# Grouped-query scores of a four-layer attention stack: two key heads on the two halves of TensorE's rows instead of one product with zero-padded keys

## The chip, the core and the metric

The kernel runs on one core of a Trainium2 chip. The metric is the device time of one execution, in microseconds (us), as the median of several runs. Durations of single instructions come from one further execution, the profiled one, taken by the hardware profiler. In its lines PE is TensorE's matmul side, PEld its weight loads, DVE is VectorE, ACT is ScalarE, POOL is GpSimd, and SP is the engine whose queue issues the DMAs; a suffix q (SPq, PEq) means the engine's sequencer.

## What is computed

The reference runs four cross-attention layers one after the other on 8 batches of 256 tokens, 512 wide, with a context of 256 tokens per batch. Layer 0 is attention with a feed-forward block, layer 1 is single-head attention, layer 3 is 16-head attention with a gate. The change is in the third of the four, layer 2, grouped-query attention: 32 query heads of 16 dimensions share 8 key/value heads, four query heads to each key head.

```python
q = hidden_state @ Wq + bq;  k = encoder_hidden_state @ Wk + bk;  v = encoder_hidden_state @ Wv + bv
q = q.reshape(b, l, KVH, GROUPS, HD).transpose(0, 2, 3, 1, 4)      # KVH 8, GROUPS 4, HD 16
k = k.reshape(b, s, KVH, HD).transpose(0, 2, 1, 3)
v = v.reshape(b, s, KVH, HD).transpose(0, 2, 1, 3)
scores = jnp.einsum('bkgld,bksd->bkgls', q, k) * scale
scores = scores + encoder_attention_mask[:, :, None, :, :]
attn = jax.nn.softmax(scores, axis=-1)
out = jnp.einsum('bkgls,bksd->bkgld', attn, v)
x = out.transpose(...).reshape(b, l, H) @ Wo + bo + hidden_state   # then a layer norm
```

## The kernel before

**Number format.** Operands of the large products are split into a high and a low part, both in the reduced format fp32r, and a product is the sum of three passes (high·high, high·low, low·high). For the 16 dimensions of a key head the three passes are stacked along the contraction: rows for (q high, k high), (q low, k high), (q high, k low), which makes 3 × 16 = 48 rows for one key head.

**Units.** Layer 2 is worked in 32 units (class `Gqa`), four for each batch; a unit takes two key heads, u = 0 and 1, and the four query heads h of each. It has these parts:

- `load` (L1252, L1253) brings the query tile `qs` (tag stack, 96 rows x 4 x 256) and the key tile `ks` (96 rows x 2 x 256) from the DRAM buffers `q2d` and `k2d`. Row 32·s + 16·u + d holds pass s, key head u, dimension d. In `ks` the columns are two blocks of 256 keys, one for each u, and the rows of the other head are zero in each block. So one product over 96 rows gives, for 128 queries of each head in the weights, 512 columns: 256 scores for u = 0 and 256 for u = 1.
- `A(h)` (L1262) makes the scores with queries on the partitions, only to find row maxima: two products 96x128 by 96x512, one for each half of the queries, each into a PSUM bank of its own (tag sm, two banks). Then DVE (L1272) adds the mask and takes the maximum, four instructions of 128x256.
- `B` (L1293 to L1296) transposes the negated maxima on TensorE, copies them out on ACT and writes them by a DMA, `stack<-mT`, into rows 96 to 99 of `qs`. Rows 96 to 99 of `ks` hold ones for the own head and zeros for the other, so the next product subtracts the maximum.
- `C(i)` (L1315) makes the scores again with keys on the partitions: for i = 0..3 (half of the keys, pair of query heads) one product 100x128 by 100x512 for each u, into the two banks of tag st. DVE (for u = 0) or ACT and POOL (for u = 1) add the mask, and one ACT instruction takes exp.
- `AV` (L636, called from `D`) multiplies the probabilities by the values: sixteen products of 128x32 by 128x512 in fp32, four at a time side by side in four groups of 32 columns of the array. `Burst` keeps them together.

**Order.** `pipeline` runs step t with A of unit t, B of unit t-1, C of unit t-2 and `AV` of an older one; each step has four slots, and in a slot A(i) and C(i) come one right after the other, followed by "fillers": products of layers 1, 2 (projections), and 3 that other generators supply, by a budget of 9 us a step. For the steps 2 to 25 `keep_order` pins TensorE's order to the order of the program; outside them a scheduler with a timeline of its own decides. All DMAs are issued in order by SP's queue.

**Preparation.** `k2d` is four buffers of 96 x 4 x 2 x 256, filled with zeros at the start of the layer: a POOL memset (L1074) of a tile of the ring `ws`, and four DMAs (L1076). `Context.kv` then writes the 16 nonzero rows of each block, six DMAs a batch (L1129). Before the units start, the two `ks` tiles are set to zero (L1557) and their rows of ones are brought by eight DMAs (L1560); rows 96 to 127 of four query tiles are set to zero (L1562).

Of the kernel before, what the change touches and what calls it, by code (L numbers as in the profile page):

```python
# [8 lines left out]
F = mybir.dt.float32  # L9
# [9 lines left out]
P = 128  # L19
# [29 lines left out]
def S(s):  # L49

    o = []
    for p in s.split(","):
# [7 lines left out]
             h="b9-10", xt="c0-3", bc="c4-5", m="c6-8")  # L60
A0_SB = dict(stack="a12-15", wc="a0-1", w8="a2-5", x8="a10-11", at="a6-7", stg="b3,b4,b6",
             P="b5,b0-2", V="v1,v0", vo="b7", nat="b8,b9", h="b10", hc="c0-3", xt="c4-7", bc="c8")
# [13 lines left out]
def tile_xattn_stack(  # L76
# [31 lines left out]
    nc = tc.nc  # L108
# [11 lines left out]
    def nm(s):  # L120
        uid[0] += 1
        return f"{s}_{uid[0]}"
# [40 lines left out]
    def dram(shape, name):  # L163
        return tc.dram_tile(shape, F, name=nm(name))

    def fp(ap):
        return ap.bitcast(F)
# [68 lines left out]
    def feat_mm(pt, ws, ft, xs, n=D):  # L236
        run(feat_steps(pt, ws, ft, xs, n))
        return 12 * n * MMUS

    def tok_mm(pt, xs, tt, ws, n=D):  # L240
        run(tok_steps(pt, xs, tt, ws, n))
        return 12 * n * MMUS
# [236 lines left out]
    v0d = [dram([P, 2, 768], "v0d") for _ in range(NB)]  # L479
    v3d = [dram([P, 2, 768], "v3d") for _ in range(NB)]  # L480


    q2d = [[dram([2, 96, 4, 256], "q2d") for _ in range(2)] for _ in range(NB)]
    k2d = [dram([96, 4, 2, 256], "k2d") for _ in range(4)]
    avd = [[dram([P, D], "avd") for _ in range(4)] for _ in range(NB)]
    med = [dram([P, 2, 2, D], "med") for _ in range(2)]
    wkvd = dram([P, 2, 2, D], "wkvd")
# [25 lines left out]
    for i in range(2):  # L513
        for o, stg, tag in ((wk, sws[i], "wk"), (xs0, sxs[i], "xs")):
            t = ph1.T([P, 2, 2, D], R, tag)
# [29 lines left out]
    def col(name, i):  # L545
        return cols(name)[:, i : i + 1]
# [77 lines left out]
    def flat(t):  # L624
        return fp(t).rearrange("p h t -> p (h t)")
# [215 lines left out]
    def stacks(ph, tag, n):  # L841
        o = []
        for _ in range(n):
            t = ph.T([P, 2, 4, 256], R, tag)
            o += [t[:, 0], t[:, 1]]
        return o
# [215 lines left out]
    ph5, ph6 = Phase(L_SB, PH_PS), Phase(L3_SB, PH_PS)  # L1062
# [5 lines left out]
    for x_ in range(2):  # L1068
        nc.sync.dma_start(
            out=w2od.rearrange("(c r x) n -> x c r n", r=16, x=2)[x_],  # L1070
            in_=w2o.rearrange("(c x r) n -> x c r n", x=2, r=16)[x_],
        )
    zero = ph5.T([96, 2048], F, "ws")
    nc.gpsimd.memset(zero, 0.0)  # L1074
    for t in k2d:
        nc.sync.dma_start(out=t.rearrange("r f u t -> r (f u t)"), in_=zero)  # L1076


    keep = {}

    def kept(tag):
        if tag not in keep:
            keep[tag] = ph5.T([P, WORDS[ph5.sb[tag][0][0]]], F, tag)
        return keep[tag]


    class Context:
# [30 lines left out]
        def kv(self):  # L1118
            b, xs = self.b, self.xs
            pt = ph5.PS("pp")  # L1120
            c = feat_mm(pt, self.wk, 0, xs, n=256)
            nat = ph5.T([P, 2, 2, 256], R, "nat")
            hi, lo = nat[:, 0, 0, :], nat[:, 0, 1, :]
            nc.scalar.activation(hi, pt[:, 0:256], AF.Identity, bias=col("bk2", 0))
            nc.vector.scalar_tensor_tensor(lo, pt[:, 0:256], col("bk2", 0), fp(hi), ALU.add, ALU.subtract)
            for s, j in enumerate((0, 0, 1)):
                for u in range(2):
                    r = 32 * s + 16 * u
                    nc.sync.dma_start(  # L1129
                        out=k2d[b % 4][r : r + 16, :, u, :].rearrange("d f t -> (d f) t"),  # L1130
                        in_=fp(nat[64 * u : 64 * u + 64, 0, j]),
                    )
            yield c
            pt = ph5.PS("pp")
            for kt in range(2):
                c = tok_mm(pt[:, kt * P : (kt + 1) * P], xs, kt, self.wv, n=P)
            tag = ("V", "vb", "va", "V4")[b % 4]
            vo = kept(tag)[:, 1024:] if tag[0] == "v" else kept(tag)
            self.vo = vo.rearrange("p (k v d) -> p k v d", k=2, v=8)
            nc.gpsimd.memset(self.vo[:, :, :, 16:32], 1.0)  # L1140
            for kt in range(2):
                nc.vector.tensor_tensor(
                    self.vo[:, kt, :, 0:16],
                    pt[:, kt * P : (kt + 1) * P].rearrange("p (v d) -> p v d", d=16),
                    bvr.rearrange("p (v d) -> p v d", d=16),
                    ALU.add,
                )
            yield 2 * c
# [90 lines left out]
    class Gqa:  # L1239
# [9 lines left out]
        def load(self):  # L1249
            self.qs, self.ks = self.st.next(), self.kst.next()  # L1250
            b, (f2, i) = self.b, divmod(self.ft, 2)
            nc.sync.dma_start(out=flat(self.qs)[0:96], in_=q2d[b][f2][i].rearrange("r h t -> r (h t)"))  # L1252
            nc.sync.dma_start(out=fp(self.ks)[0:96], in_=k2d[b % 4][:, self.ft])  # L1253


        def A(self, h):
            ph = self.ph
            if h == 0:
                self.mx = ph.T([P, 2, 4, 2], F, "mx")
            pts = [ph.PS("sm") for _ in range(2)]  # L1260
            for qt in range(2):
                nc.tensor.matmul(  # L1262
                    pts[qt],
                    lhsT=self.qs[0:96, h, qt * P : (qt + 1) * P],
                    rhs=self.ks[0:96].rearrange("p u k -> p (u k)"),
                    start=True,
                    stop=True,
                )
            for qt in range(2):
                for u in range(2):  # L1270
                    t = pts[qt][:, u * 256 : (u + 1) * 256]
                    nc.vector.tensor_tensor_reduce(  # L1272
                        out=t,
                        in0=t,
                        in1=self.am[:, qt, :],
                        scale=1.0,
                        scalar=-3.0e38,
                        op0=ALU.add,
                        op1=ALU.max,
                        accum_out=self.mx[:, u, h, qt : qt + 1],  # L1280
                    )
            if h == 3:
                self.mhl = ph.T([P, 2, 2, 8], R, "mhl")
                m3 = self.mx.rearrange("p u h q -> p u (h q)")
                nc.vector.tensor_scalar(self.mhl[:, :, 0, :], m3, -1.0, None, ALU.mult)
                nc.vector.scalar_tensor_tensor(
                    self.mhl[:, :, 1, :], m3, -1.0, fp(self.mhl[:, :, 0, :]), ALU.mult, ALU.subtract
                )

        def B(self):  # L1290
            ph = self.ph
            mp = ph.PS("pp")
            nc.tensor.transpose(mp[0:32, 0:P], fp(self.mhl.rearrange("p u j c -> p (u j c)")), ident)  # L1293
            mT = ph.T([32, P], R, "mT")
            nc.scalar.copy(mT, mp[0:32, 0:P])
            nc.sync.dma_start(out=flat(self.qs)[96:100], in_=fp(mT))  # L1296


        def probs(self):
# [7 lines left out]
        def C(self, i):  # L1307
            ph = self.ph
            kt, hp = divmod(i, 2)
            if i == 0:  # L1310
                self.ps = []
            p = self.probs()
            for u in range(2):
                pt = ph.PS("st")
                nc.tensor.matmul(  # L1315
                    pt,
                    lhsT=self.ks[0:100, u, kt * P : (kt + 1) * P],
                    rhs=self.qs[0:100, 2 * hp : 2 * hp + 2, :].rearrange("p h t -> p (h t)"),
                    start=True,
                    stop=True,  # L1320
                )
                am = self.amT[:, kt, :].unsqueeze(1).to_broadcast([P, 2, 256])
                p3 = pt.rearrange("p (h t) -> p h t", h=2)
                if (i, u) in POOL_ADDS:
                    nc.scalar.copy(p[:, u], p3)
                    last["pool"] = nc.gpsimd.tensor_tensor(p[:, u], p[:, u], am, ALU.add).ins  # L1326
                else:
                    nc.vector.tensor_tensor(p[:, u], p3, am, ALU.add)
            pf = p.rearrange("p u h t -> p (u h t)")
            last["act"] = nc.scalar.activation(pf, pf, AF.Exp).ins  # L1330
            self.ps.append(p)
# [220 lines left out]
    st = stacks(ph5, "stack", 2)  # L1552
    kst = [ph5.T([P, 4, 256], R, "ks") for _ in range(2)]
    one = const.tile([4, 256], F, name="one")
    nc.gpsimd.memset(one, 1.0)
    for t in kst:
        nc.gpsimd.memset(fp(t), 0.0)  # L1557
        for i in range(4):
            u = i % 2
            nc.sync.dma_start(out=fp(t)[96 + 2 * u : 98 + 2 * u, i, :], in_=one[0:2])  # L1560
    for t in st:
        nc.gpsimd.memset(fp(t[96:P]), 0.0)  # L1562
    ring2 = Ring(st)
    ringk = Ring([t[:, 2 * i : 2 * i + 2] for t in kst for i in range(2)])
    ring3 = Ring([])
    units = [Gqa(ring2, ringk, b, ft) for b in range(NB) for ft in range(4)]
    units += [Mha(ph6, ring3, b, ft, q3d, k3d, None) for b in range(NB) for ft in range(4)]
# [152 lines left out]
```

## Time and profile before

| what | value |
|---|---|
| device time, median of 3 runs | 1733.98 us (1725.89 to 1737.41) |
| the profiled execution's own time | 1749.12 us |
| its span, first to last instruction | 1747.3 us |
| TensorE busy, matmuls | 1608.8 us (92%), 9984 |
| TensorE busy, weight loads | 1231.5 us (70%), 9984 |
| DVE / ACT / POOL busy | 1063.5 (61%) / 877.1 (50%) / 772.0 (44%) us |
| stretch of layer 2's units | about 830 to 1450 us of the span |

In the timeline a row holds neighbouring instructions of one group: start, length from the first start to the last end, engine, line, operation, output and inputs, weights and moving operand (rows*columns, then rows x columns), count, and in brackets the idle time before with what ended it. A matmul's length includes its way through the array, so neighbouring matmuls overlap in time; the time that a product takes from the stream is read from one start to the next. In the rows of waits the columns are the total in us, how many times, and the longest.

### The profile page before, as it was taken

To read this page: it belongs to the slowest core of one execution; us is meant where nothing else is said; L and a number is where in the kernel's file an instruction comes from. 1 tells how busy PE (TensorE), PEld (TensorE's weight loads), DVE (VectorE), ACT (ScalarE), POOL (GpSimd) and SP (SyncE) were. 2 spreads that over 40 slices of the span, in tenths; PEclk is the share of its full clock that TensorE was granted. 3 is DMA by queue.
4 is the path that set the end of the run, shared out by engine and by line. 5 is a ranking of instruction groups with operands and counts; after the bars stand their busy time and mean duration, and the time that the engine had idled before them with its cause. 6 is when DMAs were issued, how large, how long until landed. Compare 5 with 4: busy or idle time off the path is not lost. (4 is left out here: it accounts for less than half of the span.)

```text
span 1747.3 us, 28325 instructions
## 1 busy us (share of the span) xinstructions
PE 1608.8 (92%) x9984; PEld 1231.5 (70%) x9984; DVE 1063.5 (61%) x2380; ACT 877.1 (50%) x1563; POOL 772.0 (44%) x792
## 2 busy tenths in 40 slices
PE   7999998999899999998889989989878999999998
PEld 6877866777667778887666767667556676778765
DVE  5258556777757766632547767767776774644353
ACT  5335545554545565642346655555564555444454
POOL 6345144323465565532225546555564564312111
PEclk9999998999989999999899999999988899999999
DMA  8879675555542534257657467466264656766562
GB/s 295 310 237 295 208 238 186 165 163 163 171 128 77 176 109 150 80 211 239 219 182 235 162 209 237 159 222 199 93 214 137 202 171 208 231 198 212 183 198 66
DMA packets 168444, 329.16 MB, mean 188 GB/s; under 512 B 16336, under 2 KB 84336, under 8 KB 162800
## 3 DMA queue, kind: packets, MB, share of 16 engines
q1 hardware_dynamic: 168304, 327.35, 58.5%
q8 instruction: 80, 1.31, 0.3%
q14 instruction: 60, 0.49, 0.1%
HBM read 230.79 MB, written 96.49 MB: 187 GB/s over the span
## 5 line engine op out<-in xcount | busy, mean ns | idle before, releaser
L688 DVE TENSOR_REDUCE negm<-sm 128x2 f32<-128x512 f32 x256 | 168.9, 682 | 114.2 <-PE sm L681 113.5
L725 ACT ACTIVATE P<-st 128x512 f32<-128x512 f32 x256 | 144.7, 594 | 111.5 <-PE st L717 108.0
L212 PE MATMUL pp<-ys,fw 128*128 128x512 f32 x768 | 192.6, 401 | 7.4 <-ACT fw L178 3.8
L226 PE MATMUL pp<-pw,gs 128*128 128x512 f32 x768 | 192.0, 397 | 2.9 <-ACT gs L1027 2.6
L636 PE MATMUL av<-P,V 128*32 128x256 f32 (+1 forms) x2204 | 173.7, 408 | 6.0 <-ACT P L1330 3.2
L212 PEld LDWEIGHTS pp<-ys,fw 128*128 128x128 f32 x768 | 145.0, 192 | 42.0 <-ACT fw L178 4.0
L212 PE MATMUL pp<-x,wq 128*128 128x256 f32 x1152 | 160.3, 288 | 9.8 <-ACT wq L181 6.3
L226 PEld LDWEIGHTS pp<-pw,gs 128*128 128x128 f32 x768 | 141.1, 188 | 38.2 <-ACT gs L1027 3.8
L212 PEld LDWEIGHTS pp<-x,wq 128*128 128x128 f32 x1152 | 148.9, 192 | 20.4 <-ACT wq L181 7.3
L1272 DVE CUSTOM_DVE_ANT_0 sm<-sm,va 128x256 f32<-128x256 f32 x256 | 104.0, 443 | 61.6 <-PE sm L1262 61.1
L1272 DVE CUSTOM_DVE_ANT_0 sm<-sm,vb 128x256 f32<-128x256 f32 x256 | 103.9, 443 | 49.2 <-PE sm L1262 48.9
L1028 POOL TENSOR_TENSOR gs<-xt,gs 128x512 fp32r<-128x512 f32 x64 | 91.9, 1444 | 85.7 <-ACT gs L1027 85.7
L1262 PE MATMUL sm<-ks,stack 96*128 96x512 f32 x256 | 101.5, 462 | 17.6 <-DVE mx L1272 7.2
L636 PEld LDWEIGHTS av<-P,V 128*32 128x32 f32 x2204 | 62.5, 110 | 61.8 <-issue 19.5
L226 PE MATMUL pp<-wo,at 128*128 128x512 f32 x384 | 103.2, 404 | 1.3 <-POOL at L1373 0.9
L1023 DVE SCALAR_TENSOR_TENSOR xt<-xt,xt 128x512 f32<-128x512 f32 x64 | 67.5, 1059 | 60.5 <-ACT xt L1022 60.5
L1315 PE MATMUL st<-stack,ks 100*128 100x512 f32 x256 | 88.2, 419 | 14.0 <-DMA stack<-mT 7.7
L693 POOL CAST mhl<-negm 128x8 fp32r<-128x8 f32 x64 | 16.2, 254 | 189.6 <-DVE negm L688 189.6
L1330 ACT ACTIVATE P<-P 128x1024 f32<-128x1024 f32 x77 | 81.4, 1058 | 33.0 <-POOL P L1326 32.9
L179 POOL TENSOR_TENSOR fw<-stg,fw 128x1024 fp32r<-128x1024 f32 x32 | 81.7, 2560 | 35.9 <-ACT fw L178 20.9
L1262 PEld LDWEIGHTS sm<-ks,stack 96*128 96x128 f32 x256 | 47.5, 201 | 63.2 <-issue 50.7
L226 PEld LDWEIGHTS pp<-wo,at 128*128 128x128 f32 x384 | 70.2, 191 | 20.4 <-POOL at L1373 3.1
(215 smaller groups left out, 3622.1 us busy)
## 6 DMA issues: line engine op xcount, KB each, us to landing
stg<-in_wfc_dram SPq DMA_DIRECT2D x32, 512.0 KB
stg<-in_wpr_dram SPq DMA_DIRECT2D x32, 512.0 KB
ws<-med SPq DMA_DIRECT2D x16, 1024.0 KB
ws<-mnd SPq DMA_DIRECT2D x16, 1024.0 KB
q2d<-nat SPq DMA_DIRECT2D x48, 256.0 KB
stack<-q2d SPq DMA_DIRECT2D x32, 384.0 KB
k0d<-nat SPq DMA_DIRECT2D x16, 512.0 KB
stack<-k0d SPq DMA_DIRECT2D x32, 256.0 KB
```

Of the source, the lines that this page charges most:

```text
L179: lo.tensor_tensor(w[:, 1], stg, fp(w[:, 0]), ALU.subtract)
L212: nc.tensor.matmul(pt[:, :n], lhsT=sel(ws, wj, kc)[:, ft * P : (ft + 1) * P], rhs=sel(xs, xj, kc), start=(k == 0), stop=(k == 11),)
L226: nc.tensor.matmul(pt[:, :n], lhsT=sel(xs, xj, kc)[:, tt * P : (tt + 1) * P], rhs=sel(ws, wj, kc), start=(k == 0), stop=(k == 11),)
L636: self.prev = nc.tensor.matmul(o, lhsT=lhsT, rhs=rhs, start=start, stop=stop, skip_group_check=True).ins
L688: nc.vector.tensor_reduce(self.negm[:, 2 * h : 2 * h + 2], pt.rearrange("p (q k) -> p q k", q=2), AX.X, ALU.max, negate=True)
L725: nc.scalar.activation(p, pt, AF.Exp)
L1023: nc.vector.scalar_tensor_tensor(v, v, 1.0 / GA, u, ALU.add, ALU.mult)
L1028: nc.gpsimd.tensor_tensor(lo, u, fp(hi), ALU.subtract)
L1262: nc.tensor.matmul(pts[qt], lhsT=self.qs[0:96, h, qt * P : (qt + 1) * P], rhs=self.ks[0:96].rearrange("p u k -> p (u k)"), start=True, sto ...
L1272: nc.vector.tensor_tensor_reduce(out=t, in0=t, in1=self.am[:, qt, :], scale=1.0, scalar=-3.0e38, op0=ALU.add, op1=ALU.max, accum_out=self. ...
L1315: nc.tensor.matmul(pt, lhsT=self.ks[0:100, u, kt * P : (kt + 1) * P], rhs=self.qs[0:100, 2 * hp : 2 * hp + 2, :].rearrange("p h t -> p (h ...
L1330: last["act"] = nc.scalar.activation(pf, pf, AF.Exp).ins
```

## The change

Each of the two key heads gets its own 48 rows: u = 0 at partitions 0 to 47, u = 1 at partitions 64 to 111 of `qs` and `ks`. Their products are issued with a tile of 64 rows by 128 columns, at row 0 or row 64 of the array (in the built program: tile size 64x128, position 0 or 64; before: 128x128, position 0).

- `k2d` becomes 2 x 48 x 4 x 256 and holds no zeros; the memset and the four DMAs of zeros are gone, and the `ws` ring is used once less. The memsets of `ks` and of the query tiles are gone too.
- `load` issues four DMAs in place of two (48 rows each). `B` issues two DMAs for the maxima in place of one, to rows 48 and 49 of each half.
- `A(h)` issues four products 48x128 by 48x256 (query half 0: u = 0, u = 1; query half 1: u = 0, u = 1) in place of two 96x128 by 96x512. A bank now holds both query halves of one u.
- `C(i)` issues its two products, now 50x128 by 50x512, both before any of their readers; the banks are taken together.

```diff
-    k2d = [dram([96, 4, 2, 256], "k2d") for _ in range(4)]
+    k2d = [dram([2, 48, 4, 256], "k2d") for _ in range(4)]
...
-    zero = ph5.T([96, 2048], F, "ws")
-    nc.gpsimd.memset(zero, 0.0)
-    for t in k2d:
-        nc.sync.dma_start(out=t.rearrange("r f u t -> r (f u t)"), in_=zero)
...
         def load(self):
-            nc.sync.dma_start(out=flat(self.qs)[0:96], in_=q2d[b][f2][i].rearrange("r h t -> r (h t)"))
-            nc.sync.dma_start(out=fp(self.ks)[0:96], in_=k2d[b % 4][:, self.ft])
+            for u in range(2):
+                nc.sync.dma_start(
+                    out=flat(self.qs)[64 * u : 64 * u + 48],
+                    in_=q2d[b][f2][i].rearrange("(s u r) h t -> u s r (h t)", s=3, u=2)[u],
+                )
+                nc.sync.dma_start(out=fp(self.ks)[64 * u : 64 * u + 48], in_=k2d[b % 4][u, :, self.ft])
...
         def A(self, h):
             for qt in range(2):
-                nc.tensor.matmul(
-                    pts[qt],
-                    lhsT=self.qs[0:96, h, qt * P : (qt + 1) * P],
-                    rhs=self.ks[0:96].rearrange("p u k -> p (u k)"),
-                    start=True,
-                    stop=True,
-                )
-            for qt in range(2):
                 for u in range(2):
-                    t = pts[qt][:, u * 256 : (u + 1) * 256]
+                    nc.tensor.matmul(
+                        pts[u][:, qt * 256 : (qt + 1) * 256],
+                        lhsT=self.qs[64 * u : 64 * u + 48, h, qt * P : (qt + 1) * P],
+                        rhs=self.ks[64 * u : 64 * u + 48],
+                        start=True,
+                        stop=True,
+                    )
+            for u in range(2):
+                for qt in range(2):
+                    t = pts[u][:, qt * 256 : (qt + 1) * 256]
                     nc.vector.tensor_tensor_reduce(
...
         def B(self):
-            nc.sync.dma_start(out=flat(self.qs)[96:100], in_=fp(mT))
+            for u in range(2):
+                nc.sync.dma_start(out=flat(self.qs)[64 * u + 48 : 64 * u + 50], in_=fp(mT)[16 * u : 16 * u + 16])
...
         def C(self, i):
+            pts = [ph.PS("st") for _ in range(2)]
             for u in range(2):
-                pt = ph.PS("st")
+                r = slice(64 * u, 64 * u + 50)
                 nc.tensor.matmul(
-                    pt,
-                    lhsT=self.ks[0:100, u, kt * P : (kt + 1) * P],
-                    rhs=self.qs[0:100, 2 * hp : 2 * hp + 2, :].rearrange("p h t -> p (h t)"),
+                    pts[u],
+                    lhsT=self.ks[r, kt * P : (kt + 1) * P],
+                    rhs=self.qs[r, 2 * hp : 2 * hp + 2, :].rearrange("p h t -> p (h t)"),
                     start=True,
                     stop=True,
                 )
+            for u in range(2):
+                pt = pts[u]
...
     for t in kst:
-        nc.gpsimd.memset(fp(t), 0.0)
-        for i in range(4):
-            u = i % 2
-            nc.sync.dma_start(out=fp(t)[96 + 2 * u : 98 + 2 * u, i, :], in_=one[0:2])
-    for t in st:
-        nc.gpsimd.memset(fp(t[96:P]), 0.0)
+        for i in (0, 2):
+            for u in range(2):
+                nc.sync.dma_start(out=fp(t)[64 * u + 48 : 64 * u + 50, i, :], in_=one[0:2])
     ring2 = Ring(st)
-    ringk = Ring([t[:, 2 * i : 2 * i + 2] for t in kst for i in range(2)])
+    ringk = Ring([t[:, 2 * i] for t in kst for i in range(2)])
```

More of the change, by code (lines that the diff above doesn't have):

```diff
@@ L1127, in kv @@
                 for u in range(2):
-                    r = 32 * s + 16 * u
                     nc.sync.dma_start(
-                        out=k2d[b % 4][r : r + 16, :, u, :].rearrange("d f t -> (d f) t"),
+                        out=k2d[b % 4][u, 16 * s : 16 * s + 16].rearrange("d f t -> (d f) t"),
                         in_=fp(nat[64 * u : 64 * u + 64, 0, j]),
```

## The prediction, made before the changed kernel had run

> **What bounds the kernel now.** The page first: TensorE is busy nearly throughout, every other engine at most 61%.
>
> ```profile
> PE 1608.8 (92%) x9984; PEld 1231.5 (70%) x9984; DVE 1063.5 (61%) x2380; ACT 877.1 (50%) x1563; POOL 772.0 (44%) x792
> PE   7999998999899999998889989989878999999998
> ```
>
> The change lies in layer 2's units, so next the sums by stage. The stage takes 620 us; TensorE is busy for 552.88 of them (0.89), DVE for 425.91 (0.69).
>
> ```profile
> 830.00:1450.00 620.00, 552.88 (x3062) 403.69 (x3063) 425.91 (x1453) 330.28 (x561) 330.69 (x332) 0.93 0.58 189
> ```
>
> So about nine tenths of a change in TensorE's work here reach the end; fillers keep it fed. The groups (page, part 5) give the two products that change:
>
> ```profile
> L1262 PE MATMUL sm<-ks,stack 96*128 96x512 f32 x256 | 101.5, 462 | 17.6 <-DVE mx L1272 7.2
> L1315 PE MATMUL st<-stack,ks 100*128 100x512 f32 x256 | 88.2, 419 | 14.0 <-DMA stack<-mT 7.7
> ```
>
> Their busy time holds the way through the array. What a product takes from the stream is read from the timeline, start to start, where nothing waits:
>
> ```profile
> 1002.24 0.64 PE L1262 MATMUL sm<-ks,stack 96*128 96x512 f32 x2
> 1002.72 0.62 PE L1315 MATMUL st<-stack,ks 100*128 100x512 f32 x2
> 1003.18 3.01 PE L212 MATMUL pp<-x,wq 128*128 128x256 f32 x24
> 1006.02 0.64 PE L1262 MATMUL sm<-ks,stack 96*128 96x512 f32 x2
> 1006.50 0.62 PE L1315 MATMUL st<-stack,ks 100*128 100x512 f32 x2
> 1006.96 2.79 PE L226 MATMUL pp<-ws,cx 128*128 128x128 f32 x24
> 1009.59 0.27 PE L1293 MATMUL pp<-ident,mhl 128*32 128x128 f32 x1
> ```
>
> A's 512 columns take (1002.72 - 1002.24)/2 = 0.24 us, C's (1003.18 - 1002.72)/2 = 0.23, 256 columns (1006.02 - 1003.18)/24 = 0.118, and 128 columns (1009.59 - 1006.96)/24 = 0.11: the short ones are held by the loads of 128 weight columns, at 0.11 each. The only tiled products in the trace are AV's, four groups of 32 columns:
>
> ```profile
> 1271.06 0.27 PE L1293 MATMUL pp<-ident,mhl 128*32 128x128 f32 x1
> 1271.26 0.62 PE L636 MATMUL av<-pk,vb 128*32 128x512 f32 x2
> 1271.27 0.62 PE L636 MATMUL av<-P,vb 128*32 128x512 f32 x2
> 1271.71 0.60 PE L636 MATMUL av<-pk,vb 128*32 128x512 f32 x2
> ...
> 1272.58 0.60 PE L636 MATMUL av<-pk,vb 128*32 128x512 f32 x2
> 1273.11 0.73 PE L1262 MATMUL sm<-ks,stack 96*128 96x512 f32 x2
> 1273.68 0.62 PE L1315 MATMUL st<-stack,ks 100*128 100x512 f32 x2
> ```
>
> Four start within 0.02 us and the next four 0.43 later: tiles do run side by side. But entering costs something: AV starts 0.20 after a product of 128 columns (0.11 alone), so +0.09. Leaving costs more: 1272.58 to 1273.11 is 0.53 (0.43 among themselves), +0.10, and the next pair of A takes 0.57 instead of 0.48, +0.09. The weight loads say why:
>
> ```profile
> 1272.15 0.12 PEld L636 LDWEIGHTS av<-pk,vb 128*32 128x32 f32 x2
> 1273.11 0.30 PEld L1262 LDWEIGHTS sm<-ks,stack 96*128 96x128 f32 x2 [0.84 <-issue]
> ```
>
> No load for A goes ahead during the last AV products; it begins when the array has run empty. Call it 0.19 a switch.
>
> **The change, part by part.** Streams first. A: before 256 x 0.24 = 61.4 us; after, 512 products of 256 columns in 256 pairs, 0.118 a pair if the halves run together: 30.2. That is -31.2. C: before 256 x 0.23 = 58.9; after, 256 products, of which 28 stand alone in the order of TensorE's instructions of the changed program (the scheduler puts something between the two), so 114 pairs and 28 single ones, 142 x 0.23 = 32.7: -26.2. The second tile starts 0.007 behind the first (AV's 0.02 over four): 159 runs, +1.1. Streams together: -56.3.
>
> Switches: that order holds 159 runs of row-tiled products; the pinned slots keep A(i) and C(i) together. 28 runs follow AV directly, where a switch is paid before too, and 3 lead into AV; so 131 entries and 156 exits are new. An exit, as after AV, costs 0.19. An entry into rows is not in the trace: the nearest rows are AV's entry (0.09 and 0.02 for 32 weight columns) and, for the exposed load of 128 columns, the exit's 0.09 to 0.10; I take 0.19. Lower bound nothing: L1293 is a product of 32 weight columns and goes in after full ones without a gap. Upper bound 0.11 more, a second load in turn. 287 x 0.19 = 54.5, less 44 exits into transposes, whose weight loads are 0.14 rather than 0.19 us long: 44 x 0.04 = 1.8. Switches: +52.7.
>
> Here a rule decides more than the row. "TensorEngine Tiling (Array Packing)" of the Trainium skill, section "Key Properties", says that changing the tiling mode drains TensorE, and that different tiles load and multiply in parallel. By the first half every run pays, and the streams' gain is spent; without it the sum would keep -56. The trace shows the drain at AV, not at L1293, and of row tiles nothing. A second rule speaks against the change: "TensorE: Matmul & The Clock Gate", "What overlaps and what doesn't", lets a weight load overlap a running product only when its row group differs. By it the second load into the same half would be bare, an estimated 0.1 for each of 242 second rounds, +24. AV's rows differ: loads start at 1272.15 with the products of their own column groups, and the next ones follow at 0.43 with no delay. The sum goes by the row.
>
> Around it. DVE's first maximum now waits for the third product of a slot instead of the first, about 0.19 + 2 x 0.118 = 0.43 instead of 0.24 us after the slot's start: +0.19, hidden by DVE's idle 31% except where TensorE waits for DVE in turn:
>
> ```profile
> PE st L1315 <- DMA stack<-mT: 7.7, 3, 4.9
> PE sm L1262 <- DVE mx L1272: 7.2, 11, 1.5
> PE sm L1262 <- DMA stack<-q2d: 2.8, 1, 2.8
> ```
>
> 11 x 0.2 = +2.2 (between 0 and the same for all 128 slots, 25). The second DMA of `B` is queued behind the first on SP, whose issue takes 0.69 (median of L1296): 3 waits, +2.1; between 0, the mask and filler work covering it, and 32 x 0.69 = 22 if every unit waited. `load` adds an issue each of 0.34 (L1252) and 0.43 (L1253): one wait, +0.8 (0 to 25 likewise). SP issues for 197 of 620 us in the stage; the 46 us added leave it below half, and behind them wait only avd, nd, h2d and weight DMAs with slots to spare. The zeros removed: a memset of 1.81 us, six of about 0.95, four DMA issues of 0.35 to 0.80 us; one load of `ws` waited 12.8 us for them on SP, while TensorE ran the feed-forward block and lost 1.4 to `ws<-med`. -1.4, between 0 and all its 4.2 idle before L212 `cx,ws`; the shifted `ws` ring within the same 4.2, either sign; I take 0, since the phase after it reuses its slots late. C's joint banks: nothing, both were taken in this order before; cover gone, one wait of the 4.2 us on `ACT P L1325`.
>
> Sum: -56.3 + 52.7 = -3.6 on TensorE, +2.2 + 2.1 + 0.8 - 1.4 = +3.7 around it: +0.1. Against the profiled execution's 1749.12 (span 1747.3 and 1.8 around it), that is 1749.2. That execution was 15.1 us longer than the median of the runs, 1733.98; on the median's scale I forecast 1734.0.
>
> **The rivals.** *The weight loads of the two halves go one after the other* (ends slower). For: loads of 128 columns in full mode do (0.11 each, L226 above). Against: AV's first eight loads start within 0.04 us (1271.26 to 1271.30). A full run has six loads: 6 x 0.11 + 0.23 = 0.89 after the drain, instead of 0.10 + 2 x 0.118 + 0.23 = 0.57. As 0.21 for each of 128 slots of A and 0.11 for each of 114 pairs of C that is +39, nine tenths of it +35: 1769. It decides (beyond 1%) once the second load shows about half of its 0.11.
>
> *Row tiles need no drain, or a cheap one* (faster). For: L1293. Against: AV, both ways. Streams alone: -56.3 x 0.89 = -50: 1684; half the price of a switch, 1708.
>
> *The halves don't overlap at all*, so the change does not do what it says. For: no row of the trace shows row tiles. Against: column tiles overlap fully. A: 512 x 0.118 = 60.4, C as before, switches paid: +52 and the 3.7: 1789.
>
> **How the numbers follow.** Chances: forecast 0.45, loads in turn 0.25, cheap switch 0.20, no overlap 0.10. The forecast's own range is 1717 to 1752 (the bounds of the small terms, which do not all fall on one side). The whole range runs from 1692 to 1775: it leaves out the fullest form of the cheap switch (0.07) and no overlap with the worst of loads in turn (0.13). About 1% is what a measurement of this kernel can tell from no change. Faster by more: 0.18 from the cheap switch and 0.03 from the forecast's edge, 0.21. Slower: 0.22 from loads in turn, 0.10, and 0.04 from the edge, 0.36. Within: 0.43.
>
> **What would show it.** In the timeline of a pinned slot: the two halves' products starting 0.01 apart (overlap), pairs of A 0.12 apart (if 0.22, loads in turn), the first product of the run 0.09 late and bare of its load, the product after the run 0.19 late. The run of A4 C2 should take 0.85 from the last full product's end to the next full one's first column, against 0.94 now. Wrong if the busy time around L1262 falls with no gap at its edges, if the waits on `mT` or on DVE grow beyond a few us, or if the clock granted in the stage (0.93) moves.

## The result, and the profile after

The changed kernel takes 1810.09 us (median; 1800.41 to 1811.82), the kernel before 1735.70. The recorded ratio, taken over all runs, is 1.0423, 95% interval 1.0361 to 1.0484 (the quotient of the two medians is 1.043). The changed kernel is slower by about 74 us, outside the range of the forecast (1734.0; 1692 to 1775). The profiled execution has a span of 1808.7 us.

From the page and the sums by stage of the changed kernel (the columns as before: window, length, busy time of PE, PEld, DVE, ACT, POOL; granted clock, which is the share of TensorE's full clock that the profile reports as granted; share of the DMA engines, GB/s):

```profile
PE 1631.4 (90%) x10240; PEld 1212.3 (67%) x10240; DVE 1062.6 (59%) x2380; ACT 879.8 (49%) x1563; POOL 767.4 (42%) x785
PE   7999989999799999996777988879869899999998
PEclk9999999999899999997888989879889799999999
```

```profile
830.00:1450.00 620.00, 511.71 (x2928) 338.43 (x2928) 376.99 (x1338) 300.17 (x506) 290.82 (x285) 0.85 0.50 165
```

The dip is in the middle of the page's PE row, in the stage of the change. In the same 620 us TensorE is now busy for 511.71 instead of 552.88, at a granted clock of 0.85 instead of 0.93, and the engines of the DMAs move 165 GB/s instead of 189: every engine stands idle more. The groups of the two products are cheaper, as meant (before: 101.5 us of busy time for A, 88.2 for C):

```profile
L1260 PE MATMUL sm<-ks,stack 48*128 48x256 f32 x512 | 88.7, 356 | 23.5 <-DVE mx L1270 16.6
L1315 PE MATMUL st<-stack,ks 50*128 50x512 f32 x256 | 72.1, 444 | 24.4 <-ACT P L1327 10.4
```

A pinned run in the timeline, where before two rows of 0.64 and 0.62 stood:

```profile
1001.98 0.87 PE L226 MATMUL pp<-wo,at 128*128 128x512 f32 x3
1002.78 0.55 PE L1260 MATMUL sm<-ks,stack 48*128 48x256 f32 x4
1003.13 0.44 PE L1315 MATMUL st<-stack,ks 50*128 50x512 f32 x2
1003.50 0.66 PE L1206 MATMUL pp<-ident,p 128*128 128x128 f32 x4
```

And the same kind of run, start by start, from the trace's records (us):

```
1007.483 load  A u=0      1007.486 load  A u=1
1007.484 A u=0            1007.488 A u=1          halves 0.004 apart
1007.591 load  A u=0      1007.594 load  A u=1    loads 0.003 apart, 0.108 after the first
1007.708 A u=0            1007.711 A u=1          second pair 0.224 after the first
1007.825 C u=0            1007.829 C u=1          C 0.117 after that
1008.157 L212             1008.382 L212           next full products: 0.332, then 0.225 instead of 0.118
```

The halves run side by side, products and loads; in 64 of 87 such runs the first two products start less than 0.01 us apart. The second pair comes 0.224 after the first; the forecast had named 0.22 as the sign of loads in turn, but the loads stand side by side, and C follows A at 0.117. It is the bare load after entering, which the price of a switch contained; another follows after leaving. So in these runs the array does what the sum said. What has grown are waits. TensorE's, ACT's and SP's in the stage of the changed kernel (engine, line, what ended the wait; total, times, longest):

```profile
PE av L635 <- ACT P L1332: 20.2, 7, 5.7
PE sm L1260 <- DVE mx L1270: 16.6, 15, 1.7
PE av L635 <- ACT pk L1332: 12.1, 4, 5.0
PE st L1315 <- ACT P L1327: 10.4, 3, 5.4
```

```profile
ACT cx L178 <- DMA nat<-in_ctxT_dram: 33.0, 6, 6.9
ACT nat L417 <- DMA k2d<-nat: 31.1, 4, 9.1
```

```profile
SPq L1362 <- DMA avd<-xt: 106.2, 28, 9.0
```

The same waits before:

```profile
PE av L636 <- ACT P L1330: 8.5, 7, 2.9
PE av L636 <- ACT pk L1330: 7.0, 4, 2.1
SPq L1360 <- DMA avd<-xt: 65.9, 32, 4.7
```

ACT waited 11.7 us on `in_ctxT` before, and 17.9 us at the four places of L417 (7.6 put down to `k2d<-nat`, 10.3 to `ks<-k2d`). One of these places shows how the waits hang together. In the changed kernel:

```profile
1115.62 0.47 ACT L417 ACTIVATE nat<-pp,bq 128x256 fp32r<-128x256 f32 x1 [7.37 <-DMA k2d<-nat]
1115.99 1.04 ACT L1332 ACTIVATE P<-P 128x1024 f32<-128x1024 f32 x1
1117.09 1.07 PE L635 MATMUL av<-P,va 128*32 128x512 f32 x2 [4.31 <-ACT P L1332]
```

The same place before (the second of the four, before the same AV):

```profile
1078.50 0.48 ACT L417 ACTIVATE nat<-pp,bq 128x256 fp32r<-128x256 f32 x1 [3.55 <-DMA k2d<-nat]
1078.88 1.05 ACT L1330 ACTIVATE P<-P 128x1024 f32<-128x1024 f32 x1
1079.97 0.62 PE L636 MATMUL av<-P,va 128*32 128x512 f32 x2 [0.19 <-ACT P L1330]
```

A projection's copy (L417) needs a buffer `nat` that a DMA out of it still reads. It waits 7.4 us instead of 3.6; behind it on ACT's queue stands the exponential; behind that AV, and TensorE stands 4.3 us instead of 0.2. The last four DMAs out of `nat` land no more slowly than before (3.0 to 4.3 us after their issue; before 3.4 to 4.6), but they are issued later: SP stood 3.95 us at a late `avd` in front of them, before 1.49. So a transfer that is not part of the change lands late, and holds what stands behind it on SP's queue. The trace's completion records say why. A DMA leaves one record for each of the 16 DMA engines that took part, and, if there were fewer, one at its issue. The times are us after the issue; the two transfers after the change are slow ones of their kinds (medians 8.26 and 4.53), and a bar stands where their times jump:

```
before  L1252 stack<-q2d  2.88 2.99 3.06 3.42 3.44 3.52 3.55 3.57 3.65 3.71 3.73 3.87 3.90 3.90 3.95 4.02
after   L1246 stack<-q2d  1.16 | 12.28 12.40 12.86
before  L1356 avd<-xt     1.85 1.85 1.87 1.90 1.90 1.91 1.91 1.92 1.93 1.94 1.94 1.95 1.95 1.97 1.97 2.01
after   L1358 avd<-xt     2.08 2.18 2.19 2.44 2.45 2.46 2.52 2.52 2.52 2.53 2.58 2.59 2.63 | 5.17 5.47 6.49
```

The query load of the changed kernel was carried by 3 engines, 64 KB each (before 16 with 24 KB), and an `avd` that 16 engines carry has 13 engines early and 3 late. Such a step, of more than 0.7 us before exactly the last three records, stands in 51 of 56 key loads, 26 of 42 `q2d` and 14 of 31 `avd` transfers of the changed kernel's stage, and in none of the kernel before. The Trainium skill, "DMA: Bandwidth & Descriptors", section "Why a DMA increments its semaphore by 16 and not by 1", gives the rule: the number of engines is the largest up to 16 that divides the outermost dimension of both sides, and they are the lowest-numbered ones. The changed load's source is 3 blocks of 16 rows, its destination 48 rows: 3. The records agree in the number; which engines they were they do not say.

### The profile page after: what moved, and what is told of

The parts are those of the page before. It is cut to its first block, busy times and chain, and to the rows that moved or that the text cites. A ratio compares the mean times of both kernels' runs of the same rounds, so it can differ in the third digit from the quotient of the medians.

```text
span 1808.7 us, 28940 instructions
## 1 busy us (share of the span) xinstructions
PE 1631.4 (90%) x10240; PEld 1212.3 (67%) x10240; DVE 1062.6 (59%) x2380; ACT 879.8 (49%) x1563; POOL 767.4 (42%) x785
## 5 line engine op out<-in xcount | busy, mean ns | idle before, releaser
L226 PE MATMUL pp<-pw,gs 128*128 128x512 f32 x768 | 195.7, 401 | 3.4 <-ACT gs L1026 2.8
L1260 PEld LDWEIGHTS sm<-ks,stack 48*128 48x128 f32 x512 | 54.6, 203 | 88.3 <-DVE mx L1270 35.3
L1260 PE MATMUL sm<-ks,stack 48*128 48x256 f32 x512 | 88.7, 356 | 23.5 <-DVE mx L1270 16.6
L1315 PE MATMUL st<-stack,ks 50*128 50x512 f32 x256 | 72.1, 444 | 24.4 <-ACT P L1327 10.4
```

Of the source, the lines that this page charges most:

```text
L226: nc.tensor.matmul(pt[:, :n], lhsT=sel(xs, xj, kc)[:, tt * P : (tt + 1) * P], rhs=sel(ws, wj, kc), start=(k == 0), stop=(k == 11),)
L1260: nc.tensor.matmul(pts[u][:, qt * 256 : (qt + 1) * 256], lhsT=self.qs[64 * u : 64 * u + 48, h, qt * P : (qt + 1) * P], rhs=self.ks[64 * u ...
L1315: nc.tensor.matmul(pts[u], lhsT=self.ks[r, kt * P : (kt + 1) * P], rhs=self.qs[r, 2 * hp : 2 * hp + 2, :].rearrange("p h t -> p (h t)"), s ...
```

## The experiments

Ratios are to the kernel before on the same chip, with 95% intervals; the clock is the median over the timed executions (before: 0.963).

| kernel | ratio | clock |
|---|---|---|
| all changed DMAs, products as before | 1.0420 (1.0396 to 1.0444) | 0.940 |
| changed products, DMAs as before | 1.0103 (1.0083 to 1.0123) | 0.950 |
| row of the maxima in two DMAs only | 1.0016 (0.9998 to 1.0035) | 0.961 |
| changed kernel, keys in one DMA | 1.0529 (1.0503 to 1.0555) | 0.926 |
| query load (3 x 16) only | 1.0504 (1.0465 to 1.0543) | 0.940 |
| all changed DMAs, rows 16 x 3 | 0.9999 (0.9982 to 1.0016) | 0.961 |
| changed kernel, rows 16 x 3 | 1.0106 (1.0082 to 1.0130) | 0.947 |
| C alone on two halves | 1.0160 (1.0123 to 1.0198) | 0.950 |
| A alone on two halves | 1.0102 (1.0070 to 1.0134) | 0.957 |
| second bank's maxima first | 1.0012 (0.9992 to 1.0032) | 0.963 |
| half the columns, no tiles | 0.9901 (0.9866 to 0.9937) | 0.950 |
| lower half of the rows only | 1.0206 (1.0177 to 1.0235) | 0.953 |
| kernel before, `nd` read 32 x 4 | 0.9907 (0.9875 to 0.9939) | 0.965 |
| changed kernel, rows 16 x 3 and `nd` read 32 x 4 | 1.0050 (1.0024 to 1.0075) | 0.951 |

**DMAs or products.** The first kernel is the one before with the changed DMAs: this edit, the keys in two loads of 48 rows too (one plain block of rows each), and the row of the maxima in two.

```diff
-            nc.sync.dma_start(out=flat(self.qs)[0:96], in_=q2d[b][f2][i].rearrange("r h t -> r (h t)"))
+            for u in range(2):
+                nc.sync.dma_start(
+                    out=flat(self.qs)[48 * u : 48 * u + 48],
+                    in_=q2d[b][f2][i].rearrange("(s u r) h t -> u s r (h t)", s=3, u=2)[u],
+                )
```

> The kernel before with the changed kernel's DMAs alone: 64 loads for a unit's tiles in two pieces each and two DMAs for the maxima, 96 DMAs more on SP's queue; products, zero rows and results as before. Queue theory (the extra DMAs delay everything behind them on SP's one queue, ACT then stands at a late buffer and the value products come late): nearly the whole loss is here, 1790 to 1815 us. Product theory (the 64-row products with their drains and later readers cost it): 1730 to 1745. A sum of both halves would be about 1770.

The second is the one before with the changed kernel's loops of A and C on the rows that lie there (so on wrong data, for the time alone); the third only splits the row of the maxima.

```diff
-                    lhsT=self.qs[0:96, h, qt * P : (qt + 1) * P],
+                    lhsT=self.qs[64 * u : 64 * u + 48, h, qt * P : (qt + 1) * P],
...
-                    lhsT=self.ks[0:100, u, kt * P : (kt + 1) * P],
+                    lhsT=self.ks[r, 0, kt * P : (kt + 1) * P],
```

> The kernel before with the changed kernel's products alone: A and C as 64-row tiles at rows 0 and 64, same counts and shapes, but reading the rows that lie there in the old layout, so the scores are of other rows, and exp is given a scale of 0.001 to stay finite; DMAs and zeros as before. Queue theory: 1720 to 1745, since streams and switches nearly cancel. Product theory: 1790 to 1815.

```diff
-            nc.sync.dma_start(out=flat(self.qs)[96:100], in_=fp(mT))
+            for u in range(2):
+                nc.sync.dma_start(out=flat(self.qs)[96 + 2 * u : 98 + 2 * u], in_=fp(mT)[16 * u : 16 * u + 16])
```

> The kernel before with only the DMA of the maxima split in two, 32 DMAs more. Queue theory: about a third of the loss of all 96, 1750 to 1765, more if the late maxima are what matters. Product theory: 1730 to 1740.

1.0420, 1.0103, 1.0016: nearly all of the loss is the DMAs', and it isn't the mere number of small ones. The products' 1.0% is left for later.

**Fewer DMAs.** The changed kernel with both halves' keys (and the rows of ones) in one DMA of 114 rows; the main line of the edit:

```diff
-                nc.sync.dma_start(out=fp(self.ks)[64 * u : 64 * u + 48], in_=k2d[b % 4][u, :, self.ft])
+            nc.sync.dma_start(out=fp(self.ks)[0:114], in_=k2d[b % 4][0:114, self.ft])
```

> The changed kernel with the key tile brought by one DMA of 114 rows instead of two of 48 (the DRAM buffer keeps ones in rows 48 to 63 of each half), 32 DMAs fewer in the units. Queue theory: a third of the loss comes back, 1780 to 1795. Product theory: unchanged, 1800 to 1815.

It is slower than the changed kernel (1.0529 against 1.0423), with 32 DMAs less, and outside both expectations. So the number of issues does not make the loss. Its trace points to the engines: this load of 114 rows has 7 records, one at the issue and 6 engines, of which three are late (2.50, 2.50, 2.59 and 7.82, 8.03, 9.09 us). 114 is divisible by 6 and by nothing above it up to 16; by the rule above, three of the six are the query load's.

**Engines or number.** One kernel has the query load (3 x 16, the edit of the first diff) alone; one has all the changed DMAs, in number and size, with the rows in the order u, r, s, so that the source's outermost dimension is 16; one is the changed kernel with that order. The query load's line (the keys' buffer gets the same order):

```diff
-                    in_=q2d[b][f2][i].rearrange("(s u r) h t -> u s r (h t)", s=3, u=2)[u],
+                    in_=q2d[b][f2][i].rearrange("(s u r) h t -> u r s (h t)", s=3, u=2)[u],
```

> The kernel before with one part of the change alone: load of the query rows as in the changed kernel, two DMAs of 48 rows whose source is three blocks of 16 rows (3 x 16 x 4 KB). Keys, row of the maxima and all products as before. Theory 'few engines': in the changed kernel each of these loads was reported by 3 DMA engines (4 completion records, the first of them at the issue) where the load before was reported by 16, and every other transfer of the stage had three late engines of 16; so this load alone carries nearly all of what all the changed DMAs cost together (1.042): 1.035 to 1.045. Rival 'more DMAs': the loss comes from issues on the sync engine and from the rotation of completion semaphores; 32 of the 96 added DMAs are here, so a third to a half of the loss: 1.012 to 1.02.

> The kernel before with all the DMAs of the changed kernel in number and size (queries and keys in two loads of 48 rows each, row of the maxima in two), but with the rows in another order, so that the outermost dimension of each load's source is 16 rows of 3 instead of 3 blocks of 16. Products as before. Theory 'few engines': the loads are reported by 16 engines again and the loss goes: 0.999 to 1.006. Rival 'more DMAs': number and size are those that cost 1.042 in the first round, so 1.035 to 1.045 again; if it is the time of one issue (0.75 us against 0.33), then as much of it as the issue keeps.

> The changed kernel with the same order of rows (16 x 3 instead of 3 x 16 in both loads of the scores); products, banks and number of DMAs as in the changed kernel. Theory 'few engines': what is left over the kernel before is what the products alone cost (1.0103): 1.005 to 1.015. Rival 'more DMAs': stays at the changed kernel's ratio of 1.042. By the terms of the forecast without the loads: 1.000.

The query load alone costs 1.0504, no less than all the changed DMAs (1.0420); with 16 engines the same DMAs cost nothing (0.9999), and the changed kernel falls to 1.0106, the cost of its products. Medians from issue to the last record, in us, of the DMAs issued between 830 and 1440 us of each span:

```
                     before   after   query load only   DMAs 16 x 3   changed, 16 x 3
query load             3.88    8.26        9.00             3.59           3.83
key load               4.16    7.62        9.04             3.42           3.49
q2d<-nat               4.04    6.78        6.81             3.65           3.31
avd<-xt                2.88    4.53        4.90             2.90           2.87
```

Not every transfer is later: `nd<-avd`, on 4 engines, takes 4.57 us in the changed kernel's stage and 4.72 before.

SP's largest wait in the kernel with the query load alone, and then in the changed kernel with rows 16 x 3:

```profile
SPq L1364 <- DMA avd<-xt: 111.8, 28, 9.3
```

```profile
SPq L1362 <- DMA avd<-xt: 64.3, 28, 4.6
```

One issue of the load in the order 16 x 3 still takes SP 0.60 us (changed 0.75, before 0.34), and 64 are issued instead of 32: the issues are hidden, as the forecast held, and the landing was not. Why the query load alone costs a little more than with the other changed DMAs was not followed up.

**The products.** One of the two products at a time, with the second kernel's edits:

> The kernel before with the second score product alone (C) issued to the two halves of the rows, keys of 50 rows; the first product (A) and every DMA as before. The products read other rows and the exponential is taken of a thousandth of its argument, so the values are not the reference's. By the forecast's prices: streams -26, 142 runs that now stand alone, 114 new entries and 142 exits at 0.19 each, +49: +22 on TensorE, nine tenths of it +20, ratio 1.012; then the tiled first product would be worth about -2 to -4 on top, and the 1.0103 of both together is made of these prices. Rival 'late maxima': the loss of the two products together is that of the first one (its maxima wait for the third product of a slot, and both of its banks are held until the last); then C alone stays below 1.004.

> The kernel before with the first score product alone (A) issued to the two halves of the rows; C and every DMA as before. The products read other rows and the exponential is taken of a thousandth of its argument, so the values are not the reference's. By the forecast's prices: streams -31, 128 runs of A alone with an entry and an exit of 0.19 each, +49, less some 5 where AV stands next to them: +12 on TensorE, +11 of it at the end, +2 for the later maxima: ratio 1.007. Rival 'late maxima': the forecast's +2 for DVE is some +10 instead, so 1.012.

1.0160 and 1.0102; both together 1.0103. Each alone makes a run of its own with an entry and an exit; together they share them. In time the prices' order held, each ratio 0.003 to 0.004 above its forecast. In the stage's work on TensorE (table below) C alone adds 20.8 us, close to the forecast (22), and A alone 22.0, where 12 was forecast. Whether later maxima were the rest needed a test by itself:

```diff
-            for qt in range(2):
+            for qt in (1, 0):
                 for u in range(2):
                     t = pts[qt][:, u * 256 : (u + 1) * 256]
```

> The kernel before with one edit: vector engine takes the maxima of the second bank first. So the first maximum waits for the second product of the slot (0.24 us later), and the bank that the next slot's first product needs is freed last; products, DMAs and switches as before. It imitates the later maxima of the changed kernel by themselves. Theory 'late maxima': TensorE's waits on the maxima grow by about 10 us as they did in the changed products (7.2 to 16.9): 1.004 to 1.008. By the forecast's term, 11 waits of 0.2: 1.001.

1.0012, the forecast's size: "late maxima" as a cause falls. TensorE's waits on the maxima stay at 7.1 us. Then the gain without the switches, and the switches without the gain (one line of each edit):

```diff
-                    rhs=self.ks[0:96].rearrange("p u k -> p (u k)"),
+                    rhs=self.ks[0:96, 0],
```

```diff
-                    lhsT=self.ks[0:100, u, kt * P : (kt + 1) * P],
+                    lhsT=self.ks[0:50, u, kt * P : (kt + 1) * P],
```

> The kernel before with the streams' gain alone: both score products take 256 columns instead of 512, in full mode, so that TensorE has the same time of columns as with two halves side by side but no change of tiling; what follows reads the same 256 columns twice, and the exponential is taken of a thousandth of its argument. Half of the scores is left out, the rest of the work stays. By the forecast's price: 512 products 0.118 instead of 0.24 and 0.23, -60, nine tenths of it -54: ratio 0.969. Rival 'clock': with less in its stream TensorE is granted half the clock more often, and waits more for the maxima; then a third or more of the gain is lost: 0.978 to 0.99 with a mean clock of 0.955 or less.

> The kernel before with the switches alone: both score products run on the lower half of the array's rows only (48 and 50 rows, 512 columns, one after the other), so every run of them changes the tiling as in the changed kernel and nothing runs beside it. The other half of the rows is left out of the sums, and the exponential is taken of a thousandth of its argument. By the forecast's price: 131 entries and 159 exits that are new, 0.19 each, less 1.8: +53 on TensorE, nine tenths of it +48: ratio 1.028, mean clock as before (0.96). Rival 'clock': the empty array at each switch costs clock beside the time itself: 1.035 to 1.045 and a mean clock of 0.953 or less; then that is where the 1% of both parts together comes from.

0.9901 and 1.0206; the two changes sum to 1.0107, and the tiled products took 1.0103 and 1.0106. The gain lies at the edge of what its rival 'clock' gave (0.978 to 0.99), far from the forecast's price (0.969); the loss is below its price (1.028). The stage, from the first A to the last C, of one profiled execution each, in us: idle time of TensorE, its busy time at the half clock, and its work, that is its busy time with half-clock time counted half (length = idle + work + half of the third column):

```
                          length   idle   busy at half clock   work
before                     614.2   66.6        73.6            510.8
DMAs 16 x 3                609.3   62.8        69.9            511.5
after                      675.7  107.9       122.7            506.5
query load only            686.0  120.7       109.0            510.8
changed, 16 x 3            620.1   59.6       104.9            508.1
changed products           618.1   66.0        77.6            513.3
half the columns           592.7   82.0        99.2            461.1
lower half of rows         631.3   37.8        95.5            545.8
A alone / C alone          617.3 / 621.8   46.7 / 48.6   75.8 / 83.2   532.8 / 531.6
```

Half the columns take 49.7 us of work off TensorE (510.8 - 461.1), but only 17.6 us off the time (1737.55 to 1719.92): idle time grows by 15, half-clock time by 26. (Idle time is 63 to 67 in the two kernels with full products and fast loads above; half-clock time varies more from execution to execution, and that of the kernel before is taken from an execution of 1749.12 us, longer than its median.) Its waits, with the order and time of the maxima as before:

```profile
PE sm L1262 <- DVE mx L1272: 16.5, 20, 1.6
PE av L636 <- ACT P L1330: 10.9, 7, 2.8
```

So waits on maxima as in the changed kernel (16.6; before 7.2) arise without later maxima, from a TensorE that is back sooner. The Trainium skill warns of it ("TensorEngine Tiling (Array Packing)", "PSUM Bottleneck": tiling speeds up TensorE and not the emptying of PSUM, which may bound next); these rows agree, with 16.5 us of waits on DVE's reading of the banks instead of 7.2.

**Better than both.** The kernel before has such a transfer itself: `nd<-avd`, 64 times 128 KB, outermost dimension 4, 5 records. Its rows in the order 32 x 4, with the rows of the projection's weights in the same order:

```diff
-            dv = avd[b][ft].rearrange("(g n r) (x t) -> n g r x t", g=4, n=2, x=2)
+            dv = avd[b][ft].rearrange("(g n r) (x t) -> n r x g t", g=4, n=2, x=2)
```

> The kernel before with one other transfer of the stage spread: the reads of numerators and denominators (nd from avd, 64 of them, 128 KB each, 4 groups outermost and 4 late engines in the trace) take their rows in the order 32 x 4 instead of 4 x 32; the rows of the projection's weights are put in the same order. Theory 'few engines': 128 KB over 4 engines is half the load per engine that the changed kernel's query rows put on 3; the four late records of the other transfers go, and what TensorE waits for late exponentials and rows of maxima falls: 0.990 to 0.999. Rival: these reads have two slots to spare and nothing that TensorE waits for stands behind them: 0.998 to 1.003.

The last kernel is the changed one with this order and the order 16 x 3 in its loads.

> The changed kernel with both few-engine transfers mended: queries and keys loaded in the order 16 x 3, numerators and denominators read in the order 32 x 4. If the two effects are independent of the products, 1.0106 x 0.9907 = 1.001 (0.997 to 1.005), that is 1% over the kernel before with the spread reads alone: the tiled products still cost about 1%, with a granted clock below that kernel's 0.964. Rival: the 1% that the products cost came from waits on transfers that are late with 4 engines, and goes with them: 0.991 or less, level with the kernel before with the spread reads.

The kernel before with `nd` spread takes 0.9907 of its time: faster than both kernels of this study. `nd` lands in 2.54 us instead of 4.72 (16 records), `avd` in 2.12 instead of 2.88, and TensorE's waits on the exponentials for AV fall from 8.5 and 7.0 to:

```profile
PE av L636 <- ACT P L1331: 3.9, 3, 1.6
PE av L636 <- ACT pk L1331: 2.9, 2, 1.6
```

Of the 171 transfers on 16 engines in the stage (`avd`, `ks`, `q2d`, `stack`, `k2d`), 28 had a step before exactly the last four records; with `nd` spread it is 1 of 172. With the changed products the ratio is 1.0050, at the upper edge of what independence gives: the products cost 1.4% beside it (1.0050 / 0.9907). Waits on the transfers with 3 and 4 engines aren't the cause of their 1%.

## Why the prediction was wrong, point by point

- **The step that failed** is the one on `load`: "`load` adds an issue each of 0.34 (L1252) and 0.43 (L1253): one wait, +0.8 (0 to 25 likewise)", with "behind them wait only avd, nd, h2d and weight DMAs with slots to spare". It priced the issue and took the transfer as before. The issue took 0.75 us and not 0.34, but the number of issues was harmless (0.9999 with 16 engines). The transfer went from 16 engines to 3, 64 KB on each, and transfers on 16 engines beside it landed late by three records: `q2d` 6.78 instead of 4.04 us, `avd` 4.53 instead of 2.88. The slots were spare only for transfers as fast as before. Price: 1.0423 / 1.0106, about 3.1%, some 54 us; and the upper bound, 25, was one by issues too. The diff showed it: a source of three dimensions with 3 outermost.
- **Streams and switches** were right as a sum, in TensorE's work: -3.6 forecast; the stage's work is 4.3 less in the changed kernel, 2.7 less with the loads mended, 2.5 more with the products alone. That is in part luck: by themselves the gain measured 49.7 (60 forecast) and the switches 35 (53), which would make -15. The halves start 0.004 us apart; no load in turn. Entering is 0.09 us late (208 ns from the last full product to the first tiled one, 119 between full ones), with a bare load behind; leaving likewise (320 against 230). The run took 0.87 us including the late second product, 0.85 forecast. The bare load shows with 512 columns too: on one half of the rows the second product of A starts 0.33 to 0.35 us after the first in 78 of 80 pinned runs. Before, 37 of 79 such runs have 0.23 to 0.25 and the rest over 0.3, so some runs were held there already. Whether that is why the switches came out smaller was not followed up.
- **"About nine tenths of a change in TensorE's work here reach the end"** failed for a gain, and with it the sum, which let -56.3 and +52.7 cancel. Of 50 us less work 18 arrived in the time of the runs, and 21.5 in the length of the profiled stage. Of the 35 us that the switches add, 36 arrived in the time, but only 17 in the profiled stage, where idle time fell by 29; that a loss comes through whole is therefore not shown. The factor was the busy share of the stage, which says how often TensorE is at work, not what comes next when it is faster. Against the forecasts for these two kernels (0.969 and 1.028) the gain fell short by 2.1% and the loss by 0.7%. Together that is the 1% that the products cost where -0.2% was forecast.
- **The clock**, named as a sign that would prove the forecast wrong, moved: 0.85 in the stage, over the whole execution 0.934 instead of 0.963. With the query load alone idle time and half-clock time grow together (54 and 35 us more); which causes which was not tested. With the products alone the clock is 0.950. The waits on DVE, named as a sign too, grew from 7.2 to 16.6.
- **DVE's later maxima** (+2.2) and **the second DMA of `B`** (+2.1) were sized well enough: 1.0012 and 1.0016, and both intervals hold 1.
- **Zeros removed** (-1.4) and **joint banks** (0) were not measured by themselves.
- **The rivals**: none of them was it. "No drain" would not have given 1684: the gain without any switch ends at 1720. The loads in turn and the missing overlap are excluded by the run above, although its 0.224 is the figure that the forecast had named for loads in turn.

## What to carry to other kernels

When a DMA is split or its rows are taken in another order, look at the outermost dimension of both sides and count the engines that it leaves; a load that gathers on three engines delayed transfers on all 16 beside it here, and the wait turned up far away, at a buffer that an unrelated copy needs. Read the price of less work on a busy engine from what it would wait for next, not from its busy share. And look for the same fault in the kernel that is there: spreading the one transfer on 4 engines gave 0.9%, where the change had been forecast to give nothing.

## What the runs showed of the hardware

- The records fit transfers over few engines that share the same ones: beside the 3-engine loads three of 16 records are late (51 of 56 key loads), beside the 4-engine reads four (13 of 42 `k2d` before), and of the six engines of the 114-row load three. The records do not name the engine.
- The granted clock halves in pieces of 3.41 us or multiples of it (23 of the 24 pieces in the trace before). In the stage the number of pieces hardly differs, 11 to 17 with full products and 11 to 16 with tiled ones (17 in the changed kernel, 18 with half the columns), but they last longer: 1.6 to 1.8 times 3.41 us on average with full products and spread loads, 1.9 to 2.5 with tiled ones, 2.1 with half the columns, 2.7 on one half of the rows, 2.8 in the changed kernel. That TensorE's thinner stream keeps the clock down longer would fit; it wasn't tested, and stays open.
